# Routed experts' results: scattered to rank and token order inside the expert loop and read by plain loads, in place of rows by slot and 32 gathers

## The chip, the cores and the metric

The kernel runs on one core of a Trainium2 chip, in one launch. The metric is the device time in microseconds (us). The core's engines are TensorE (PE, matrix products), VectorE (DVE), ScalarE (ACT), GpSimd (POOL) and SyncE (SP); each works through its own instructions in order, and semaphores hold it where it needs another engine's result or a transfer. SP and ACT issue plain DMA transfers; the indirect ones (one row per index) are issued by POOL.

## The reference

Two layers run over x (2048 tokens of 256 numbers) with a second sequence of 1601 rows as context: cross attention, a mixture of experts, a second cross attention with a gate, a second mixture. The change concerns the first mixture and the start of what follows it. With `xf` the normalised rows, that mixture is

```python
def _ffn(x, w1, w2, w3):
    return jax.nn.silu(x @ w1.T) * (x @ w3.T) @ w2.T
for i in range(2):                       # two shared experts, for every token
    shared = shared + _ffn(xf, sw1[i], sw2[i], sw3[i])
logits = xf @ router_w.T + expert_bias
rw, sel = jax.lax.top_k(logits, 2)       # two of eight experts for each token
rw = jax.nn.softmax(rw)
...
out = out + cw[:, None] * _ffn(xf, e1, e2, e3)    # for each expert; cw is 0 where not chosen
out = out + shared                       # and x = x + out
```

So each token has two chosen experts, its rank 0 and its rank 1, with weights `rw`.

## The kernel before, in words

All is float32. The 2048 tokens lie in 16 tiles of 128 (`NT = 16`; token `i*128 + p` is on partition `p`), taken in 4 blocks of 4 tiles (`NB`, `BT`). `xs` holds the running x in SBUF for the whole kernel. A scheduler in the tile framework orders each engine's instructions and sets the semaphores; a tile pool with `bufs=n` rotates n buffers, and a new tile waits for the readers of the old one.

The stages around the change, with the profile's times:

- **Norm and router (180 to 228 us).** Four blocks are normalised by DVE into `h_f` (`layernorm`, line 189) and turned by PE (line 199) into `hT_f`. 32 small products give the logits (line 508). DVE finds the two best experts of each token (lines 518 and 519) and works out a slot for each pair of token and rank (`slot`, line 580). Slots are grouped by expert, each expert's group rounded up to tiles of 128: 39 tiles (`NSLOT`).
- **Scatter (228 to 315 us).** 32 indirect transfers (line 593; loop over 16 tiles `i`, then 2 ranks `k`) put rows of `h_f` into the DRAM tensor `rows_in` at their slots. It was filled with zeros before (line 412). Each scatter waits for the one before, since all write the same tensor.
- **Shared experts (190 to 374 us), beside the scatter.** `hidden(e, b)` computes for each of 4 column groups `hc` two products of 128x512 (line 614), ACT takes silu of the first (line 619), DVE multiplies by the second (line 620). `outward` multiplies by the third weight (line 629) and DVE adds to `xs` (line 632). The products of line 614 rotate through 4 banks of PSUM, two for each `hc`, so the second product of one `hc` needs DVE's line 620 of two groups earlier.
- **Routed experts (374 to 605 us).** For each of the 39 tiles of slots: load from `rows_in` (`arrive`, line 677), turn, two products with the expert's weights (`up`, line 691), turn (line 703), third product (`down`, line 711), copy out of PSUM by DVE (`rout`, line 715), store to `rows_out` by a plain transfer that ACT issues (line 716).
- **Start of the second layer (603 to 690 us).** PE projects the context (lines 219 and 232) and folds weights (lines 780 to 814). Beside that, for each block of tokens, 8 gathers (line 830, into `g`, 6 buffers) fetch the two expert rows of each token from `rows_out` by `slot`, DVE adds them to `xs` with the weights `tw` (line 835) and normalises the block into `hr` (line 189). PE turns it (line 199), ACT copies it (line 839), and PE computes the first scores against it (line 255), which ACT copies out (line 257) and DVE takes the running maximum of (`m`, line 263).

```python
for b in range(NB):                                  # lines 825 to 843, shortened
    for j in range(BT):
        i = b * BT + j
        for k in range(2):
            nc.gpsimd.indirect_dma_start(out=g, in_=rows_out, in_offset=...slot[:, k, i : i + 1]...)
            nc.vector.scalar_tensor_tensor(xs[:, i, :], g, tw[:, i, k : k + 1], xs[:, i, :], ALU.mult, ALU.add)
    h = layernorm(b * BT, BT, prew, hr[:, b * BT : (b + 1) * BT, :])
    turn_block(ps_t, h, ...)
    scores(first_em, hT, S, qs[:, :, 0:BW], BW, None, first=b * BT, end=(b + 1) * BT)
```

Of the kernel before, what the change touches and what calls it, by code (L numbers as in the profile page):

```python
# [9 lines left out]
F32 = mybir.dt.float32  # L10
# [7 lines left out]
P = 128  # L18
# [24 lines left out]
def xattn_ffn_kernel(ctx: ExitStack, tc: tile.TileContext, t: dict, out: bass.AP):  # L43
# [30 lines left out]
        return w  # L74


    rows_in = tc.dram_tile([NSLOT * P, D], F32, name="rows_in")
    rows_out = tc.dram_tile([NSLOT * P, D], F32, name="rows_out")

    rows_sub = tc.dram_tile([SC, 2 * D], F32, name="rows_sub")  # L80

# [1 line left out]
    tw = const.tile([P, NT, 2], F32, name="tw")  # L83
    slot = const.tile([P, 2, NT], U32, name="slot")
    owner = const.tile([P, NSLOT], I32, name="owner")
    zero = const.tile([P, D], F32, name="zero")
    ident = const.tile([P, P], F32, name="ident")
    ones = const.tile([P, P], F32, name="ones")

# [222 lines left out]
    with ExitStack() as ph:  # L312
# [82 lines left out]
        for b in range(NB + 1):  # L395
            new = between = None
            if b + 1 < NB:
                h = rows_before(b + 1)
            if b < NB:
                qT, past = ready.pop(b)  # L400
                e, m = em = score_tiles(pools)
                scores(em, kT, SC, qT, BW, None)
                acc = sp.tile([P, BW], F32, name="acc")

                def each(r, k0, k1, b=b, e=e, acc=acc):
                    for k in range(k0, k1):
                        if k == 1:
                            add = nc.gpsimd.tensor_tensor(acc, e[:, 0, :], e[:, 1, :], ALU.add)
                            if b == 0:
                                with tc.issue_after(add.ins):  # L410
                                    nc.gpsimd.memset(zero, 0.0)
                                nc.sync.dma_start(
                                    rows_in.rearrange("(n p) d -> p n d", p=P),
                                    zero.unsqueeze(1).to_broadcast([P, NSLOT, D]),
                                )
                        elif k:
                            nc.gpsimd.tensor_tensor(acc[:r, :], acc[:r, :], e[:r, k, :], ALU.add)

                between = shift_exp(pools, e, m, SC, BW, each)
                new = (b, e, acc, past)  # L420
            if last is None:
                project(ps_m, wv0, ctxT, 0, 3, lambda i, r, ps: copy(i, v[:r, i, :], ps))
                next(between)
                project(ps_m, wv0, ctxT, 3, 6, lambda i, r, ps: copy(i, v[:r, i, :], ps))
                next(between)
                project(ps_m, wv0, ctxT, 6, NCT, lambda i, r, ps: copy(i, v[:r, i, :], ps))
            else:
                n, e, acc, past = last
                ov = bank(ps_m)
                for k, r in enumerate(parts_of(SC)):  # L430
                    if between is not None and k in (3, 7):
                        next(between)
                    nc.tensor.matmul(ov, v[:r, k, :], e[:r, k, :], start=(k == 0), stop=(k == NCT - 1))  # L433
                oT = sp.tile([P, BW], F32, name="oT")
                nc.scalar.copy(oT, ov)
                dps = bank(ps_s)
                for j in range(BT):
                    nc.tensor.matmul(
                        dps[:, j : j + 1], acc[:, j * P : (j + 1) * P], ones[:, 0:1], start=True, stop=True
                    )  # L440
                rden = sp.tile([P, BT], F32, name="rden")
                nc.vector.reciprocal(rden, dps[:, 0:BT])
                after(n, oT, rden, past)
            if b + 1 < NB:
                ready[b + 1] = before(b + 1, h)
            last = new
# [47 lines left out]
    with ExitStack() as ph:  # L494
# [1 line left out]
        work = sbuf(ph, "f0w", 2, "right")  # L496
        acts = sbuf(ph, "f0a", 2, "right")

        h = keep.tile([P, NT, D], F32, name="h_f")
        hT = keep.tile([P, DC, S], F32, name="hT_f")  # L500
        for b in range(NB):
            hb = layernorm(b * BT, BT, work, h[:, b * BT : (b + 1) * BT, :])
            turn_block(ps_t, hb, lambda c, tp: copy(c, hT[:, c, b * BW : (b + 1) * BW], tp))

        lg_ps = bank(ps_t)[:, : NT * NE].rearrange("p (n e) -> p n e", e=NE)
# [82 lines left out]
        nc.vector.tensor_scalar(ownf, ownf, float(NE - 1), None, ALU.min)  # L588
        nc.vector.tensor_copy(owner, ownf)

        for i in range(NT):
            for k in range(2):
                nc.gpsimd.indirect_dma_start(
                    out=rows_in, out_offset=bass.IndirectOffsetOnAxis(ap=slot[:, k, i : i + 1], axis=0),
                    in_=h[:, i, :], in_offset=None, bounds_check=NSLOT * P - 1,
                )
# [73 lines left out]
    with ExitStack() as ph:  # L670
        work = sbuf(ph, "r0w", 3)
        in_tiled = rows_in.rearrange("(n p) d -> n p d", p=P)
        out_tiled = rows_out.rearrange("(n p) d -> n p d", p=P)

        def arrive(s):
            r = work.tile([P, D], F32, name="rin")
            nc.sync.dma_start(r, in_tiled[s])
            tp = bank(ps_t)
            for c in range(DC):
                nc.tensor.transpose(tp[:, c * P : (c + 1) * P], r[:, c * P : (c + 1) * P], ident)  # L680
            rT = work.tile([P, DC, P], F32, name="rT")
            nc.vector.tensor_copy(rT.rearrange("p c q -> p (c q)"), tp[:, 0:D])
            return rT

        def up(s, rT):
            e = nc.tensor.value_load(owner[0:1, s : s + 1], min_val=0, max_val=NE - 1)
            base = nc.tensor.snap(e * (DC * HID))
            ps = [bank(ps_s) for _ in range(2)]
            for w, p in zip(routed, ps):
                for c in range(DC):  # L690
                    nc.tensor.matmul(  # L691
                        p, rT[:, c, :], w[:, bass.ds(base + c * HID, HID)], start=(c == 0), stop=(c == DC - 1)
                    )
            sl = work.tile([P, HID], F32, name="rsl")
            nc.scalar.activation(sl, ps[0], AF.Silu)  # L695
            act = work.tile([P, HID], F32, name="ract")
            nc.vector.tensor_tensor(act, sl, ps[1], ALU.mult)  # L697
            return base, act

        def turn(act):  # L700
            tp = bank(ps_t)
            for hc in range(NHC):
                nc.tensor.transpose(tp[:, hc * P : (hc + 1) * P], act[:, hc * P : (hc + 1) * P], ident)  # L703
            aT = work.tile([P, NHC, P], F32, name="raT")
            nc.scalar.copy(aT.rearrange("p c q -> p (c q)"), tp)
            return aT

        def down(s, base, aT):
            y = bank(ps_m)[:, 0:D]
            for hc in range(NHC):  # L710
                nc.tensor.matmul(  # L711
                    y, aT[:, hc, :], routed[2][:, bass.ds(base + hc * D, D)], start=(hc == 0), stop=(hc == NHC - 1)
                )
            r = work.tile([P, D], F32, name="rout")
            nc.vector.tensor_copy(r, y)
            nc.scalar.dma_start(out_tiled[s], r)

        ks = l1k.tile([P, DC, SC], F32, name="ks")
        vs = l1k.tile([P, NCT, D + 1], F32, name="vs")
        kbs = l1k.tile([P, NCT], F32, name="kbs")  # L720
        rT = {s: arrive(s) for s in range(2)}
        hid, aTs = {}, {}
        for s in range(NSLOT + 2):
            if s < NSLOT:
                hid[s] = up(s, rT.pop(s))
            if 0 <= s - 1 < NSLOT:
                base, act = hid[s - 1]
                aTs[s - 1] = turn(act)
            if s + 2 < NSLOT:
                rT[s + 2] = arrive(s + 2)  # L730
            if 0 <= s - 2 < NSLOT:
                down(s - 2, hid.pop(s - 2)[0], aTs.pop(s - 2))
            if s == 4:
                ctxT = second_layer_loads()
                nc.gpsimd.memset(vs[:, :, D : D + 1], 1.0)
# [5 lines left out]
    with ExitStack() as ph:  # L741
# [9 lines left out]
        blocks = [(0, 512), (512, 512), (1024, 256), (1280, SC - 1280)]  # L751
        pre = ExitStack()
        prew = sbuf(pre, "a1l", 2)
        gath = sbuf(pre, "a1g", 6)
        fold1 = sbuf(pre, "a1f", 1)


# [65 lines left out]
        fold_weights()  # L823

        for b in range(NB):
            for j in range(BT):
                i = b * BT + j
                for k in range(2):
                    g = gath.tile([P, D], F32, name="g")
                    nc.gpsimd.indirect_dma_start(  # L830
                        out=g, out_offset=None, in_=rows_out,
                        in_offset=bass.IndirectOffsetOnAxis(ap=slot[:, k, i : i + 1], axis=0),
                        bounds_check=NSLOT * P - 1,
                    )
                    nc.vector.scalar_tensor_tensor(
                        xs[:, i, :], g, tw[:, i, k : k + 1], xs[:, i, :], ALU.mult, ALU.add
                    )
            h = layernorm(b * BT, BT, prew, hr[:, b * BT : (b + 1) * BT, :])
            turn_block(ps_t, h, lambda c, tp: nc.scalar.copy(hT[:, c, b * BW : (b + 1) * BW], tp))
# [313 lines left out]
```

## Time and profile before

| what | value |
|---|---|
| median of 9 runs (lowest to highest) | 1145.72 us (1140.7 to 1148.41) |
| the profiled execution: its time, and its span | 1146.24 us, 1144.4 us |
| mean granted TensorE clock, share of full speed | 0.967 |
| busy share of the span: PE, DVE, ACT, POOL | 93%, 47%, 29%, 27% |
| chain that ended last, by engine | PE 73%, DVE 19%, DMA 3%, ACT 2%, issue 2% |
| the 32 scatters into `rows_in`: first to last start | 228.0 to 312.5 us |
| the 32 gathers from `rows_out`: first to last start | 606.3 to 647.5 us |

The profile is of one execution, and its times run from the span's start. The execution's time is 1.84 us more than its span, and 0.5 us above the median. Views used below are the chain of waits that ended last, tables of each engine's busy time in given stretches, lists of one engine's instructions in order of time, and the waits of one tile. In a list a row has its start, its length, the engine, the line, the operation, what it writes and reads, how often it stands there, and in brackets the idle time before it with what ended it. A matmul of 128x512 in float32 stands as two records, 0.43 us apart at full clock. Ends of matmuls are modelled, so a PE that shows busy may contain a wait.

### The profile page before, as it was taken

What the parts mean: (1) busy time and instruction counts of PE and PEld (TensorE: products, weight loads), DVE (VectorE), ACT (ScalarE), POOL (GpSimd) and SP (SyncE); (2) the same over time, 40 slices, a digit from 0 to 9 for tenths busy, and PEclk for the clock granted to TensorE, in tenths of its full rate; (3) what the DMA queues carried; (4) which work ended last, traced back from release to release, by engine and by line L of the source; (5) the groups of instructions that cost most, each with busy time, mean ns of one, the idle gap of its engine ahead of it and who ended that gap; (6) DMA issues with size and microseconds to landing.
All of it is one profiled execution on the core that took longest, in us unless ns stands there. A gap on an engine that the chain in (4) does not pass through costs nothing.

```text
span 1144.4 us, 11226 instructions
## 1 busy us (share of the span) xinstructions
PE 1066.5 (93%) x3728; PEld 654.5 (57%) x3728; DVE 541.9 (47%) x1288; ACT 330.1 (29%) x542; POOL 313.2 (27%) x298
## 2 busy tenths in 40 slices
PE   6997897999999999999999999999999965999994
PEld 3653445656566566666665644465764554575773
DVE  6677889422222222222223745441415666465664
ACT  4762532210110112221123435331305500333311
POOL 1461550033300000000006506612319998100000
PEclk9998898799999999999999999999999986999997
DMA  8410006411103111111103200000013212000000
GB/s 315 136 53 1 0 1 248 193 51 47 50 28 88 58 46 47 46 46 46 46 22 88 72 1 0 19 19 37 1 42 101 65 56 83 9 10 10 1 19 19
DMA packets 38950, 63.55 MB, mean 56 GB/s; under 512 B 6189, under 2 KB 26541, under 8 KB 38894
## 3 DMA queue, kind: packets, MB, share of 16 engines
q1 hardware_dynamic: 26686, 40.02, 10.1%
q0 software_dynamic: 5632, 16.78, 4.8%
q10 hardware_dynamic: 6576, 6.03, 1.6%
q8 instruction: 31, 0.51, 0.2%
q14 instruction: 25, 0.20, 0.1%
HBM read 43.02 MB, written 19.79 MB: 55 GB/s over the span
## 4 chain that ended last, share of the span: by engine, by line
PE 73%; DVE 19%; DMA 3%; ACT 2%; issue 2%; POOL 0%; DVEq 0%; SPq 0%; POOLq 0%; ACTq 0%
PE sc L255 17%; PE sc L691 12%; PE sc L614 10%; PE mm L898 8%; PE mm L711 6%; PE mm L629 5%; DVE e L291 3%; PE mm L306 2%; PE sc L1011 2%; PE sc L860 2%; DMA g<-rows_out,slot 2%; PE tp L703 1%; DVE st L178 1%; PE mm L433 1%; DVE newton L160 1%
## 5 line engine op out<-in xcount | busy, mean ns | idle before, releaser
L691 PE MATMUL sc<-rew,rT 128*128 x312 | 140.3, 592 | 0.6 <-DMA bvs<-in_bvs_dram 0.6
L614 PE MATMUL sc<-hT_f,ew 128*128 128x512 f32 x256 | 115.8, 608 | 0.1
L306 PE MATMUL mm<-vs,e 128*128 128x257 f32 (+1 forms) x416 | 98.9, 387 | 0.0
L291 DVE TENSOR_TENSOR e<-e,tp 128x2048 f32<-128x2048 f32 (+3 forms) x48 | 86.3, 1859 | 21.0 <-PE tp L284 21.0
L691 PEld LDWEIGHTS sc<-rew,rT 128*128 128x128 f32 x312 | 59.0, 190 | 58.7 <-issue 56.8
L294 ACT ACTIVATE e<-e 128x2048 f32<-128x2048 f32 (+3 forms) x48 | 74.2, 1571 | 63.2 <-DVE e L291 62.8
L255 PE MATMUL sc<-hT,ks 128*128 128x512 f32 (+1 forms) x208 | 91.6, 597 | 0.0
L255 PE MATMUL sc<-qs,hT 128*128 128x512 f32 (+2 forms) x256 | 88.3, 501 | 2.5 <-DVE m L263 1.6
L257 ACT COPY e<-sc 128x512 f32<-128x512 f32 (+3 forms) x116 | 61.1, 536 | 101.5 <-PE sc L255 101.3
L898 PE MATMUL mm<-e,hr 128*128 128x512 f32 (+2 forms) x256 | 88.0, 499 | 0.0
L306 PEld LDWEIGHTS mm<-vs,e 128*128 128x128 f32 (+1 forms) x416 | 78.8, 194 | 13.0 <-issue 2.5
L263 DVE TENSOR_TENSOR m<-sc,m 128x512 f32<-128x512 f32 (+3 forms) x100 | 62.6, 626 | 49.6 <-ACT e L257 46.6
L697 DVE TENSOR_TENSOR ract<-rsl,sc 128x512 f32<-128x512 f32 x39 | 26.8, 687 | 120.2 <-PE sc L691 116.8
L614 PEld LDWEIGHTS sc<-hT_f,ew 128*128 128x128 f32 x256 | 49.6, 196 | 58.1 <-issue 56.7
L711 PE MATMUL mm<-rew,raT 128*128 x312 | 73.6, 379 | 0.0
L255 PEld LDWEIGHTS sc<-qs,hT 128*128 128x128 f32 x256 | 47.8, 189 | 39.1 <-issue 26.4
L898 PEld LDWEIGHTS mm<-e,hr 128*128 128x128 f32 x256 | 48.2, 190 | 35.4 <-issue 28.2
L255 PEld LDWEIGHTS sc<-hT,ks 128*128 128x128 f32 (+1 forms) x208 | 38.6, 187 | 46.9 <-issue 46.2
L255 PE MATMUL sc<-qT,kT 128*128 128x512 f32 (+1 forms) x104 | 51.4, 649 | 13.6 <-DVE m L263 13.6
L695 ACT ACTIVATE rsl<-sc 128x512 f32<-128x512 f32 x39 | 23.3, 597 | 134.3 <-PE sc L691 134.3
L796 POOL COPY wvg<-wvc 128x256 f32<-128x256 f32 x2 | 0.7, 400 | 222.7 <-PE sc L691 222.7
L711 PEld LDWEIGHTS mm<-rew,raT 128*128 128x128 f32 x312 | 56.3, 190 | 6.1
(260 smaller groups left out, 1564.0 us busy)
## 6 DMA issues: line engine op xcount, KB each, us to landing
rew<-in_ew_dram SPq DMA_DIRECT2D x24, 512.0 KB, 10.7
rows_in<-zero SPq DMA_DIRECT2D x1, 4992.0 KB, 16.2
rin<-rows_in SPq DMA_DIRECT2D x39, 128.0 KB, 2.0
rows_out<-rout ACTq DMA_DIRECT2D x39, 128.0 KB, 1.7
ew<-in_ew_dram SPq DMA_DIRECT2D x7, 512.0 KB, 8.4
ctxT<-in_ctxT_dram SPq DMA_DIRECT2D x6, 512.0 KB, 7.8
rows_sub<-sgrow SPq DMA_DIRECT2D x12, 256.0 KB, 2.0
out_dram<-xs SPq DMA_DIRECT2D x8, 256.0 KB, 2.1
```

The costliest lines, as they stand in the source:

```text
L255: nc.tensor.matmul(ps, kT[:, d, k * P : k * P + r], q[:, d, :], start=(d == 0), stop=(d == nd - 1))
L257: nc.scalar.copy(e[:r, k, :w], ps)
L263: nc.vector.tensor_tensor(m[:r, :w], ps, upto, ALU.max)
L291: nc.vector.tensor_tensor(part, part, bc[:r, :w].unsqueeze(1).to_broadcast([r, k1 - k0, w]), ALU.add)
L294: nc.scalar.activation(part, part, AF.Exp)
L306: nc.tensor.matmul(ov[:c, : D + 1], e[:r, k, j * P : j * P + c], v[:r, k, :], start=(k == 0), stop=(k == len(rows) - 1))
L614: nc.tensor.matmul(p, w[:, c, cols], hT[:, c, b * BW : (b + 1) * BW], start=(c == 0), stop=(c == DC - 1),)
L629: nc.tensor.matmul(y, act[:, hc, j * P : (j + 1) * P], a2[:, hc, :], start=(hc == 0), stop=(hc == NHC - 1))
L691: nc.tensor.matmul(p, rT[:, c, :], w[:, bass.ds(base + c * HID, HID)], start=(c == 0), stop=(c == DC - 1))
L697: nc.vector.tensor_tensor(act, sl, ps[1], ALU.mult)
L711: nc.tensor.matmul(y, aT[:, hc, :], routed[2][:, bass.ds(base + hc * D, D)], start=(hc == 0), stop=(hc == NHC - 1))
L898: nc.tensor.matmul(ov, hr[:, k, d * P : (d + 1) * P], e[:, k, :w], start=(k == 0), stop=(k == NT - 1))
```

## The change

The row of a slot now carries its destination with it. `rows_in` is one number wider (257), and so are `h_f` and `zero`. Before the scatters of rank `k`, DVE writes the integer `k*2048 + token` into the last column of `h_f`; the loop is now over `k` first, then `i`. The zero rows carry numbers from 4096 up, a dump area. When the scatters have landed, one transfer on SP reads the 4992 single numbers of that column into `goes_to`. In the expert loop POOL scatters each tile of results to `rows_out[goes_to]`, where it was stored by slot. `rows_out` is thus in order of rank and token, and each block of 512 tokens is read by two plain transfers of 512 KB on SP (`g0` and `g1`, 2 buffers each) where there were 8 gathers.

```diff
-    rows_in = tc.dram_tile([NSLOT * P, D], F32, name="rows_in")
-    rows_out = tc.dram_tile([NSLOT * P, D], F32, name="rows_out")
+    rows_in = tc.dram_tile([NSLOT * P, D + 1], F32, name="rows_in")
+    rows_out = tc.dram_tile([2 * S + P, D], F32, name="rows_out")
...
-                                    nc.gpsimd.memset(zero, 0.0)
+                                    nc.gpsimd.memset(zero[:, 0:D], 0.0)
+                                    nc.gpsimd.iota(
+                                        zero[:, D : D + 1].bitcast(I32), pattern=[[0, 1]], base=2 * S, channel_multiplier=1
+                                    )
...
-        h = keep.tile([P, NT, D], F32, name="h_f")
+        h = keep.tile([P, NT, D + 1], F32, name="h_f")
+        place_i = keep.tile([P, 2, NT], I32, name="place_i")
+        nc.gpsimd.iota(place_i, pattern=[[S, 2], [P, NT]], base=0, channel_multiplier=1)
...
-        for i in range(NT):
-            for k in range(2):
+        for k in range(2):
+            nc.vector.tensor_copy(h[:, :, D : D + 1].bitcast(I32), place_i[:, k, :].unsqueeze(2))
+            for i in range(NT):
                 nc.gpsimd.indirect_dma_start(
                     out=rows_in, out_offset=bass.IndirectOffsetOnAxis(ap=slot[:, k, i : i + 1], axis=0),
                     in_=h[:, i, :], in_offset=None, bounds_check=NSLOT * P - 1,
...
+            nc.sync.dma_start(goes_to, rows_in.rearrange("(n p) d -> p n d", p=P)[:, :, D].bitcast(U32))
...
-            nc.sync.dma_start(r, in_tiled[s])
+            nc.sync.dma_start(r, in_tiled[s][:, 0:D])
...
-            nc.scalar.dma_start(out_tiled[s], r)
+            nc.gpsimd.indirect_dma_start(
+                out=rows_out, out_offset=bass.IndirectOffsetOnAxis(ap=goes_to[:, s : s + 1], axis=0),
+                in_=r, in_offset=None, bounds_check=2 * S + P - 1,
+            )
...
-        gath = sbuf(pre, "a1g", 6)
+        gath = sbuf(pre, "a1g", 2)
+        by_token = rows_out[0 : 2 * S, :].rearrange("(k n p) d -> p k n d", k=2, p=P)
...
         for b in range(NB):
+            got = []
+            for k in range(2):
+                g = gath.tile([P, BT, D], F32, name=f"g{k}")
+                nc.sync.dma_start(g, by_token[:, k, b * BT : (b + 1) * BT, :])
+                got.append(g)
             for j in range(BT):
                 i = b * BT + j
-                for k in range(2):
-                    g = gath.tile([P, D], F32, name="g")
-                    nc.gpsimd.indirect_dma_start(
-                        out=g, out_offset=None, in_=rows_out,
-                        in_offset=bass.IndirectOffsetOnAxis(ap=slot[:, k, i : i + 1], axis=0),
-                        bounds_check=NSLOT * P - 1,
-                    )
+                for k, g in enumerate(got):
                     nc.vector.scalar_tensor_tensor(
-                        xs[:, i, :], g, tw[:, i, k : k + 1], xs[:, i, :], ALU.mult, ALU.add
+                        xs[:, i, :], g[:, j, :], tw[:, i, k : k + 1], xs[:, i, :], ALU.mult, ALU.add
                     )
```

More of the change, by code (lines that the diff above doesn't have):

```diff
@@ L85, in xattn_ffn_kernel @@
     owner = const.tile([P, NSLOT], I32, name="owner")
-    zero = const.tile([P, D], F32, name="zero")
+    goes_to = const.tile([P, NSLOT], U32, name="goes_to")
+    zero = const.tile([P, D + 1], F32, name="zero")
     ident = const.tile([P, P], F32, name="ident")
@@ L410, in each @@
                                 with tc.issue_after(add.ins):
-                                    nc.gpsimd.memset(zero, 0.0)
+                                    nc.gpsimd.memset(zero[:, 0:D], 0.0)
+                                    nc.gpsimd.iota(
+                                        zero[:, D : D + 1].bitcast(I32), pattern=[[0, 1]], base=2 * S, channel_multiplier=1
+                                    )
                                 nc.sync.dma_start(
                                     rows_in.rearrange("(n p) d -> p n d", p=P),
-                                    zero.unsqueeze(1).to_broadcast([P, NSLOT, D]),
+                                    zero.unsqueeze(1).to_broadcast([P, NSLOT, D + 1]),
                                 )
@@ L497, in xattn_ffn_kernel @@
         acts = sbuf(ph, "f0a", 2, "right")
-        h = keep.tile([P, NT, D], F32, name="h_f")
+        h = keep.tile([P, NT, D + 1], F32, name="h_f")
+        place_i = keep.tile([P, 2, NT], I32, name="place_i")
+        nc.gpsimd.iota(place_i, pattern=[[S, 2], [P, NT]], base=0, channel_multiplier=1)
         hT = keep.tile([P, DC, S], F32, name="hT_f")
         for b in range(NB):
-            hb = layernorm(b * BT, BT, work, h[:, b * BT : (b + 1) * BT, :])
+            hb = layernorm(b * BT, BT, work, h[:, b * BT : (b + 1) * BT, 0:D])
             turn_block(ps_t, hb, lambda c, tp: copy(c, hT[:, c, b * BW : (b + 1) * BW], tp))
@@ L672, in xattn_ffn_kernel @@
         in_tiled = rows_in.rearrange("(n p) d -> n p d", p=P)
-        out_tiled = rows_out.rearrange("(n p) d -> n p d", p=P)
+        with nc.allow_non_contiguous_dma(reason="one element of each row"):
+            nc.sync.dma_start(goes_to, rows_in.rearrange("(n p) d -> p n d", p=P)[:, :, D].bitcast(U32))
         def arrive(s):
             r = work.tile([P, D], F32, name="rin")
-            nc.sync.dma_start(r, in_tiled[s])
+            nc.sync.dma_start(r, in_tiled[s][:, 0:D])
             tp = bank(ps_t)
```

## The prediction

> **What bounds the kernel.** I read the page's busy times and the chain of waits first, then the tables of stretches for the stages that the diff touches, then the lists of each engine there.
>
> ```profile
> PE 1066.5 (93%) x3728; PEld 654.5 (57%) x3728; DVE 541.9 (47%) x1288; ACT 330.1 (29%) x542; POOL 313.2 (27%) x298
> ...
> PE 73%; DVE 19%; DMA 3%; ACT 2%; issue 2%; POOL 0%; DVEq 0%; SPq 0%; POOLq 0%; ACTq 0%
> ```
>
> PE is busy 93% of the span, and the diff leaves its work as it is: it takes away transfers. So the question is where PE stands still for those. The chain gives DMA 3%, which looks like the gathers; stretches of the stage with the gathers tell what that is worth (columns: length, then busy time and count of PE, weight loads, DVE, ACT, POOL; granted clock, DMA share, GB/s):
>
> ```profile
> core 0: us, PE busy (x) PEld busy (x) DVE busy (x) ACT busy (x) POOL busy (x), PEclk, DMA share, GB/s
> 604.00:612.00 8.00, 8.00 (x20) 3.46 (x19) 1.60 (x4) 3.04 (x5) 4.49 (x5) 1.00 0.22 67
> 612.00:622.00 10.00, 10.00 (x31) 4.96 (x30) 5.03 (x15) 4.31 (x8) 7.74 (x8) 1.00 0.36 105
> ...
> 652.00:662.00 10.00, 8.11 (x25) 3.80 (x24) 8.54 (x31) 3.16 (x7) 0.00 (x0) 1.00 0.00 0
> ```
>
> PE works through the gathers without a gap until the last stretch. Who held it there, by the list of its waits between 605 and 665 and the lists of PE and DVE:
>
> ```profile
> PE sc L255 <- DVE m L263: 1.6, 1, 1.6
> PE sc L255 <- ACT hT L839: 0.6, 2, 0.3
> ```
> ```profile
> 654.62 1.98 PE L255 MATMUL sc<-qs,hT 128*128 128x512 f32 x4 [0.29 <-ACT hT L839]
> 658.21 1.98 PE L255 MATMUL sc<-qs,hT 128*128 128x512 f32 x4 [1.60 <-DVE m L263]
> ```
> ```profile
> 656.17 1.38 DVE L189 TENSOR_SCALAR hr<-xs,mv,rstd 128x256 f32<-128x256 f32 x4
> 657.47 0.68 DVE L263 TENSOR_TENSOR m<-sc,e 128x512 f32<-128x512 f32 x1
> ```
>
> The gathers pace DVE (its line 835 waits for them 24 times, 22.6 us together), DVE ends its last normalisation at 657.5, and only then comes the maximum (line 263) that frees a bank for PE. PE, not the gathers, sets the rest of the stage. In the order of instructions of the changed kernel, PE's sequence here is the same.
>
> **Term A, the read-back: -1.9.** PE's two matmuls from 654.62 take four records of 0.43, so they end at 656.34; the next starts at 658.21. 1.87 is what the gathers cost. New dates: the last three scatters of results follow one another as the old ones do (a new start each 2.68). `rout` of the last three tiles is ready at 599.66 and the two that follow; starts at 599.70, 602.38, 605.06, landing by 607.7. Eight loads of 512 KB follow on SP. The zero fill moves 4992 KB in 16.2, 315 GB/s, so 1.4 to 1.7 a load, behind a landing time of 1.7 (a 128 KB store): block 0's pair is there by 611 to 612, and the others stay ahead of DVE. DVE's work from 604 to 657.5 sums to 31.5, so it is done at 643 to 645, 12 before PE needs it. It pays from the first microsecond and ends at 1.87: PE is full before, and the two stalls of 0.29 on ACT stay.
>
> **Term B, the first copy into `h_f`: +0.2, and scatters later.** The nearest row is DVE's copy of 128x32 at line 580, 0.17; I take 0.2. It stands behind the normalisations, in a stretch where DVE is the limit:
>
> ```profile
> 180.00:200.00 20.00, 15.20 (x64) 9.49 (x63) 19.73 (x115) 5.78 (x12) 1.40 (x10) 0.83 0.89 349
> ```
>
> There the order also moves one matmul of line 614 ahead of the logits (line 508). PE loses nothing by that, but the logits, and with them slots and scatters, come 0.86 later, less some idle time that it fills: I take 0.8. The first scatter starts at 228.8 instead of 228.0.
>
> **Term C, the second copy: +2.1.** The copy for `k=1` overwrites what the 16 scatters of `k=0` read, so DVE waits for their landing. In DVE's new order it stands after the eighth line 632 of the shared experts (which ends at 264.6), and queued behind it are line 620 for `hc=0` of the next group and all after it. Line 620 frees a bank that PE needs two groups on. The lists of POOL, DVE and ACT:
>
> ```profile
> 268.64 0.97 POOL L593 DMA_INDIRECT rows_in<-h_f,slot  x1 [1.70 <-DMA rows_in<-h_f,slot]
> 271.31 0.97 POOL L593 DMA_INDIRECT rows_in<-h_f,slot  x1 [1.70 <-DMA rows_in<-h_f,slot]
> ```
> ```profile
> 264.19 0.42 DVE L632 TENSOR_TENSOR xs<-xs,mm 128x256 f32<-128x256 f32 x1 [1.30 <-PE mm L629]
> 268.06 0.69 DVE L620 TENSOR_TENSOR act<-sl,sc 128x512 f32<-128x512 f32 x1 [3.45 <-PE sc L614]
> ```
> ```profile
> 272.77 0.60 ACT L619 ACTIVATE sl<-sc 128x512 f32<-128x512 f32 x1 [2.84 <-PE sc L614]
> ```
>
> The row at 271.31 is the 17th scatter, released by the landing of the 16th, which is what the copy now waits for. So the copy starts at 271.31 + 0.8 + 16d, where d is what a row of 1028 bytes adds to a scatter's 2.71 over one of 1024. Copy 0.2, line 620 0.65: the bank is free at 272.96 + 16d. PE needs it when the first product of `hc=2` is done; silu of that starts at 272.77, as soon as it is, so 272.73. Stall: 0.2 + 16d. The trace has no write that isn't aligned to 1024, so d has bounds only. Below: 0, or a little less by chance, for 4 bytes in 1024. Above: the data movement of a scatter doubled. The queue's packets fill 13.1% of 16 engines over the 90 us with the 32 scatters, 0.37 each, so d is at most 0.37 and the stall at most 6.1. I take 0.12, nearer to the row of the same scatter than to its double: 0.2 + 1.9 = 2.1.
>
> [...]
>
> **At nothing, with their cover.** The zero fill of 257 columns (46 to 62; SP's next transfer is at 181). Loads of `rin` (median 2.0), issued two tiles of 5.82 ahead. 39 scatters on POOL in place of 39 stores on ACT: 2.68 each within 5.82 a tile, `rout` has three buffers, and PE runs through this loop without a gap. `goes_to`, 4992 single numbers, waits on SP for the last scatter (about 320). By rows: above, 4992 elements at the rate at which the load of `bvT`, 256 single elements, exceeds a plain store of 128 KB (3.1 against 1.7; 16 a DMA engine, so 0.09 each) are 312 a DMA engine, 28 us, done near 348. Behind it on SP are loads of the first routed weights, due from 360.5 on. Over 45 us would delay these and PE behind them. The scatters end some 5 later than before, near 320; `rin` is first loaded at 367.8.
>
> **The sum.** 0.2 + 2.1 - 1.9 = +0.4. The profiled execution took 1146.24 (span 1144.4), so 1146.6; it is 0.5 above the median, against which the forecast is **1146.1**.
>
> **What else moves: the clock.** The delayed logits are small products, and around them the clock is granted at half:
>
> ```profile
> 208.00:212.00 4.00, 4.00 (x21) 4.00 (x20) 0.00 (x0) 0.00 (x0) 0.00 (x0) 0.50 1.03 411
> ...
> 219.00:222.00 3.00, 3.00 (x11) 1.54 (x10) 2.22 (x11) 1.43 (x2) 0.00 (x0) 0.97 0.00 0
> ```
>
> By narrower stretches the half clock lasts from 205.5 to 219.2, 13.7 us. Moving its edges costs half of the move. A quarter of the stretch, 3.4, is worth 1.7 either way, and I carry that as noise. [...]
>
> **Rivals.**
>
> *Neither sign shows (0.42):* the forecast: the gain of A and the wait of C cancel within noise; d between 0.02 and 0.24. Its own range is 1144.2 to 1148.0.
>
> *Faster (0.20).* The scatters aren't later than before and d is near 0, so the copy is through by 271.5, line 620 before 272.73, and C is 0: 0.2 - 1.9 = -1.7. With a half-clock stretch shorter by 3.4, another -1.7: 1142.3. For it: the landing of a scatter (2.4) is mostly fixed time, 0.37 being data. Against: the moved matmul eats the slack of 0.5 alone.
>
> *Slower (0.38).* The wait of DVE at the second copy takes the place of the gathers' wait: from d above 0.24 the whole is over 0.2% slower. At 0.37 C is 6.1 and the sum 0.2 + 6.1 - 1.9 = +4.4: 1150.1; with a longer half-clock stretch 1151.8. [...] Against: so small a share of a scatter's time is data.
>
> *The read-back late, or `goes_to` over 45 us* (within the 0.38): DVE's chain would have to begin after 623 instead of 611, each microsecond beyond costing one. *That the gathers were hidden anyway* is most of the forecast: 22.6 us of DVE's waits are worth 1.9.
>
> The range is 1142.3 to 1151.8, both rivals' ends. One execution of this kernel can't be told from another within 0.2%, 2.3 us: faster by more than that 0.20, within 0.42, slower 0.38.
>
> **What would show it.** In the profile after: scatters in `rows_in` start 2.71 + d apart; DVE stands idle from about 265 to the 16th landing, with PE idle before the second product of `hc=2` at 272.7; no wait of PE on line 263 near 656; loads of `g0`, `g1` land from 611 on; `goes_to` lands before 360. Wrong would be: PE waiting for `rin` or routed weights after 360, PE waiting for block 0's `hr` before 645, or a period of scatters over 3.1.

## The result, and the profile after

The changed kernel takes 1154.13 us (median of 10 runs, 1151.54 to 1157.33) against 1145.31 for the kernel before (31 runs): a ratio of 1.008, 95% interval 1.0067 to 1.0093. It is slower by 0.8%. The forecast was 1146.1, with a range of 1142.3 to 1151.8, and had called no change that can be seen the likeliest. The profiled execution took 1152.37, its span 1150.6. Its lines have other numbers; those of the kernel before stand in brackets: scores 257 (255), maximum 265 (263), the new copies 599, scatters 601 (593), products of the shared experts 622 (614), the product on DVE 628 (620), 640 (632).

First the list of PE's waits, between 185 and 380 us and then between 605 and 665:

```profile
PE sc L622 <- DVE act L628: 5.4, 1, 5.4
PE tp L201 <- DVE h_f L191: 4.6, 1, 4.6
```
```profile
PE mm L805 <- ACT vT L796: 0.5, 1, 0.5
PE mm L827 <- ACT eT L796: 0.3, 1, 0.3
PE sc L257 <- ACT hT L851: 0.3, 1, 0.3
```

The wait on the maximum, 1.6 before, is gone (the wait of 4.6 on line 191 stood there before with 4.7). In its place PE waits 5.4 on line 628 of the shared experts. The lists of POOL, DVE and PE there show the chain that was forecast:

```profile
271.28 0.97 POOL L601 DMA_INDIRECT rows_in<-h_f,slot  x1 [2.09 <-DMA rows_in<-h_f,slot]
274.75 0.97 POOL L601 DMA_INDIRECT rows_in<-h_f,slot  x1 [2.50 <-DVE h_f L599]
```
```profile
274.11 0.18 DVE L599 COPY h_f<-place_i 128x16 int32<-128x16 int32 x1 [12.69 <-DMA rows_in<-h_f,slot]
274.21 1.28 DVE L628 TENSOR_TENSOR act<-sl,sc 128x512 f32<-128x512 f32 x2
```
```profile
274.96 8.26 PE L622 MATMUL sc<-hT_f,ew 128*128 128x512 f32 x12 [5.42 <-DVE act L628]
```

DVE stands 12.69 us ahead of the copy, until the 16th scatter (row 271.28) has landed. Two of line 628, which had been queued behind the copy, then go through in one piece, and PE resumes at 274.96. The clock did something that nobody had priced. Stretches around it (PE busy, PEld, DVE, ACT, POOL, granted clock, DMA share, GB/s):

```profile
268.00:274.00 6.00, 1.54 (x4) 0.38 (x2) 0.00 (x0) 0.00 (x0) 1.94 (x2) 0.99 0.12 44
274.00:281.00 7.00, 6.04 (x8) 2.62 (x9) 2.08 (x4) 0.60 (x1) 2.15 (x3) 0.52 0.11 38
281.00:290.00 9.00, 9.00 (x39) 6.98 (x38) 1.95 (x4) 0.60 (x1) 3.27 (x4) 1.00 0.13 46
```

By narrower stretches the half clock lasts from 273.9 to 280.7, 6.8 us. It begins while PE still stands, so PE works 5.7 us at half clock (274.96 to 280.7) and loses 2.9 of them. By this profile the second copy costs 5.4 + 2.9 = 8.3.

The other dates, by differences between the two profiles: from the last copy of `rout` to line 898 (910 now) 86.5 us before, 84.9 after; the expert loop, first to last product, 220.0 in both; from the start to its first product 376.4 and 381.7. That last difference, 5.3, is less than 8.3 since the half-clock stretch at the router is 6.8 here where it was 13.7, which is worth 3.4 the other way. These sum to +5.3 - 1.6 of the 6.2 between the spans. The rest, about 2.4, lies between line 910 and the end, whose code the change leaves as it is. In the sixteen profiles of this case that last part takes 451.8 to 457.4 us, with 36.5 to 46.2 us at half clock in it, so differences of some us between single profiles say nothing on the change.

### The profile page after: what moved, and what is told of

It reads as the page before. It is cut to its first block, busy times and chain, and to the rows that moved or that the text cites. A ratio compares the mean times of both kernels' runs of the same rounds, so it can differ in the third digit from the quotient of the medians.

```text
span 1150.6 us, 11190 instructions
## 1 busy us (share of the span) xinstructions
PE 1066.5 (93%) x3728; PEld 653.4 (57%) x3728; DVE 541.9 (47%) x1290; ACT 329.7 (29%) x542; POOL 320.0 (28%) x307
## 4 chain that ended last, share of the span: by engine, by line
PE 71%; DVE 16%; issue 7%; ACT 2%; DMA 1%; POOL 1%; DVEq 0%; POOLq 0%; SPq 0%; ACTq 0%
PE sc L257 18%; PE sc L700 12%; PE mm L910 7%; PE mm L720 6%; PE sc L622 5%; PE mm L637 4%; DVE e L293 3%; PE mm L308 2%; PE sc L1023 2%; PE sc L872 2%; PE sc L221 2%; PE tp L712 1%; PE mm L438 1%; DVE newton L162 1%; POOL rows_in L601 1%
## 5 line engine op out<-in xcount | busy, mean ns | idle before, releaser
L725 POOL DMA_INDIRECT rows_out<-rout,goes_to x39 | 38.0, 973 | 196.1 <-DVE rout L724 190.5
L308 PEld LDWEIGHTS mm<-vs,e 128*128 128x128 f32 (+1 forms) x416 | 78.9, 195 | 13.1 <-issue 2.5
L257 PEld LDWEIGHTS sc<-hT,ks 128*128 128x128 f32 (+1 forms) x208 | 38.6, 187 | 46.9 <-issue 46.2
L601 POOL DMA_INDIRECT rows_in<-h_f,slot x32 | 31.4, 981 | 106.2 <-DMA rows_in<-h_f,slot 60.5
## 6 DMA issues: line engine op xcount, KB each, us to landing
rew<-in_ew_dram SPq DMA_DIRECT2D x24, 512.0 KB, 10.2
rows_in<-zero SPq DMA_DIRECT2D x1, 5011.5 KB, 21.6
```

The lines of the kernel that those rows point to most:

```text
L257: nc.tensor.matmul(ps, kT[:, d, k * P : k * P + r], q[:, d, :], start=(d == 0), stop=(d == nd - 1))
L308: nc.tensor.matmul(ov[:c, : D + 1], e[:r, k, j * P : j * P + c], v[:r, k, :], start=(k == 0), stop=(k == len(rows) - 1))
L601: nc.gpsimd.indirect_dma_start(out=rows_in, out_offset=bass.IndirectOffsetOnAxis(ap=slot[:, k, i : i + 1], axis=0), in_=h[:, i, :], in_off ...
```

## Experiments

The kernels ran in four groups, each on a chip of its own together with the kernel before. On the first two chips that one took 1145.7 and 1145.1 us, on the last two 1160.6 and 1160.8; a ratio is always to the kernel before on the same chip.

**The second copy on POOL.**

```diff
-            nc.vector.tensor_copy(h[:, :, D : D + 1].bitcast(I32), place_i[:, k, :].unsqueeze(2))
+            (nc.gpsimd if k else nc.vector).tensor_copy(h[:, :, D : D + 1].bitcast(I32), place_i[:, k, :].unsqueeze(2))
```

> The changed kernel with one difference: the second copy into h_f (rank 1) runs on POOL, in its queue between the 16th and 17th scatter, so DVE waits for nothing there. Theory A (DVE's wait at that copy holds the bank, and the standstill of 5.4 us then costs a stretch of half clock): the scatters still start 3.0 us apart, but PE has no wait on line 628 and no half clock between 273 and 281; 5.4 + 3.4 = 8.8 us less than the changed kernel, 1143.5 to 1146 us, level with the kernel before. Theory B (the loss lies in the expert loop, in 39 scatters of results, or in the wider rows themselves): 1152 us or more. Theory C (only the standstill counts, the half clock would come anyway): 1148 to 1149.

Measured: 1146.65 us, ratio 0.9997 (0.9981 to 1.0013). PE has no wait between 200 and 340, and the same two stretches are full:

```profile
268.00:274.00 6.00, 6.00 (x17) 2.84 (x16) 0.99 (x2) 1.19 (x2) 1.78 (x3) 1.00 0.13 47
274.00:281.00 7.00, 7.00 (x33) 5.94 (x32) 2.07 (x5) 0.00 (x0) 2.92 (x3) 1.00 0.11 38
```

The scatters themselves are as slow as in the changed kernel (3.08 for the first 16). So the loss, the half clock too, hangs on DVE's wait, to within the interval of 0.16% (1.8 us) either way. The 39 scatters in the expert loop cost nothing there: the loop takes 220.0 us in all sixteen profiles, with scatters or with stores. The strided load and the wider rows cost nothing that shows. The median is 0.65 above theory A's range, with single runs from 1140.8 to 1147.9.

**The scatter side alone.**

```diff
-            nc.gpsimd.indirect_dma_start(out=rows_out, out_offset=...goes_to[:, s : s + 1]..., in_=r, ...)
+            nc.scalar.dma_start(out_tiled[s], r)
...
-                nc.sync.dma_start(g, by_token[:, k, b * BT : (b + 1) * BT, :])
+                    nc.gpsimd.indirect_dma_start(out=g, in_=rows_out, in_offset=...slot[:, k, i : i + 1]...)
```

> The scatter side of the change alone: wide rows, rank order and both copies on DVE stay, goes_to is loaded, but the results are stored by slot by ACT and read back by the 32 gathers as before. Theory A: PE's standstill of 5.4 and the half clock behind it are there as in the changed kernel, and the wait of 1.6 to 1.9 on line 265 near 656 is back: 1.9 us slower than the changed kernel, 1155 to 1157 us. Theory B (scatters of results cost something in the expert loop): faster than the changed kernel, under 1153. If the read-back was worth more than 1.9, over 1158.

Measured: 1152.9 us (6 runs), ratio 1.0068 (1.0051 to 1.0084). In the profile both waits are there, though not of the size that theory A has: 6.5 on line 628 and 1.3 on line 265, with 6.8 us of half clock at the first. The median misses: it is 1.2 below the changed kernel where 1.9 above was expected, and so just in theory B's range. What theory B would need, a longer expert loop with scatters, isn't there (220.0 us in both). The profiled execution, of 1155.8, lies in theory A's range. A gain of under 2 us can't be read from these medians.

**Rows of 272 numbers, and of 264.** Both widen `rows_in`, `h_f` and `zero`, so that each scatter writes the wider row whole, and leave the rest, the wait of DVE included.

```diff
-    rows_in = tc.dram_tile([NSLOT * P, D + 1], F32, name="rows_in")
+    rows_in = tc.dram_tile([NSLOT * P, 272], F32, name="rows_in")
```

> The changed kernel with rows of 272 numbers (1088 bytes, a multiple of 64) in rows_in, h_f and zero instead of 257 (1028 bytes); everything else as in the changed kernel, DVE's wait at the second copy too. Theory A1 (rows that begin at odd addresses land later): the scatters start 2.70 to 2.75 us apart again, the 16th lands some 4.5 us earlier against PE, PE waits under 1 us on line 628, no half clock behind it: 1143.5 to 1146.5. Theory A2 (any row longer than 1024 bytes lands later): the period stays at 3.0 or grows, 1153 or more. Theory A3 (64 bytes is not enough, only 256 or 512 would do): period 2.9 to 3.0, 1152 or more.

> The changed kernel with rows of 264 numbers (1056 bytes, a multiple of 32 but not of 64). Theory A1 with a step at 64 bytes: period of the first 16 scatters 2.9 to 3.0 as with 1028 bytes, PE waits some 5 us on line 628. With a step at 32 bytes or less: 2.70 to 2.75 and under 1 us. Theory A2: 3.0.

Measured with 272: 1142.91 us, 0.6 below the expected range, ratio 0.9989 (0.9976 to 1.0002); period of the first 16 scatters (from one start to the next) 2.73 instead of 3.04. With 264: 1144.73 in one run, period 2.73. PE's waits, first with 272 and then with 264:

```profile
PE sc L622 <- DVE act L628: 0.5, 1, 0.5
```
```profile
PE sc L622 <- DVE act L628: 0.6, 1, 0.6
```

More bytes per row, and the landing is early again, so the amount of data isn't it. Rows of 1056 bytes, a multiple of 32 and not of 64, are enough for the 2.73. Most rows of 1028 bytes neither begin nor end on multiples of 32 in DRAM; which of the two counts isn't shown, since rows that begin 1056 bytes apart with only 1028 of them written weren't run. What became longer shows in the issues and shares of DMA, first of the kernel before (225 to 315 us), then of the changed one (222 to 322):

```profile
q0 software_dynamic: 1536, 4.20, 13.1%
...
rows_in<-h_f,slot POOLq DMA_INDIRECT x32, 2.4
```
```profile
q0 software_dynamic: 1536, 4.21, 11.9%
...
rows_in<-h_f,slot POOLq DMA_INDIRECT x32, 2.7
```

13.1% of 90 us and 11.9% of 100 us, over 32 scatters, are 0.37 us each in both. In these scatters the engines move rows of 1028 bytes as fast as those of 1024; the time from issue to landing grows, from 2.4 to 2.7 in the median. The zero fill grew too: 16.2 us in rows of 1024 bytes, 20.4 to 21.6 in rows of 1028, 17.2 in rows of 1088. But there it is the engines' own time: between 44 and 70 us the fill's queue has 58.6% of the 16 engines before and 76.9% after, 15.2 and 20.0 us.

**Which side.** `h_f` padded to 264 in SBUF, `rows_in` and the length of what is written left at 257.

```diff
-        h = keep.tile([P, NT, D + 1], F32, name="h_f")
+        h = keep.tile([P, NT, 264], F32, name="h_f")
...
-                    in_=h[:, i, :], in_offset=None, bounds_check=NSLOT * P - 1,
+                    in_=h[:, i, 0 : D + 1], in_offset=None, bounds_check=NSLOT * P - 1,
```

> The changed kernel with h_f padded to 264 numbers in SBUF, while each scatter still moves 257 numbers into rows_in of 257: the rows begin at multiples of 32 bytes on the reading side only. If the writing side makes the landing later: period 2.95 to 3.1 and PE waits 5 to 6.5 us on line 628. If the reading side does: 2.70 to 2.75 and under 1 us.

Measured: period 3.14, PE's wait 6.9, 1155.56 us in one run. Rows that begin at multiples of 32 bytes on the reading side alone didn't help; it took the writing side, in DRAM, for the period of 2.73.

**More scatters ahead of the copy.** With rows of 264, a repeat of the first scatter (the same rows once more) before the second copy, once or twice:

```diff
+            for _ in range(1 if k else 0): nc.gpsimd.indirect_dma_start(out=rows_in, out_offset=...slot[:, 0, 0:1]..., in_=h[:, 0, :], ...)
             nc.vector.tensor_copy(h[:, :, D : D + 1].bitcast(I32), place_i[:, k, :].unsqueeze(2))
```

> Rows of 264 numbers (period 2.73, wait 0.6 in the run before) and one scatter more ahead of the second copy: the 16 scatters of rank 0 are followed by a repeat of the first one, so DVE waits for 17 landings. Theory A (stall = landing of the last one + 0.85 - PE's need): PE's wait on line 628 is 0.6 + 2.7 = 3.3 us. Theory B (the standstill had another cause than the number of landings that DVE waits for): 0.6 as before. Clock: if 3.3 us of standstill are enough for a stretch of half clock, one begins between 272 and 280; theory A holds either way.

> As the run with one scatter more, but two: DVE waits for 18 landings. Theory A: 0.6 + 5.4 = 6.0 us on line 628, and a half clock of 6.8 us behind it, as with the 5.4 us of the changed kernel. Theory B: 0.6 and none.

Measured: waits of 0.3 and 3.2, at 1140.79 and 1148.36 us. Both expectations missed by 3, and the list of DVE (here with two more) says why: the scheduler put the copy behind one line 628 more.

```profile
264.15 0.69 DVE L628 TENSOR_TENSOR act<-sl,sc 128x512 f32<-128x512 f32 x1 [3.45 <-PE sc L622]
274.63 0.18 DVE L599 COPY h_f<-place_i 128x16 int32<-128x16 int32 x1 [9.79 <-DMA rows_in<-h_f,slot]
```

What is now held up is the line 628 of the next column group, whose bank PE needs 3.43 us later (two products of 1.716). 0.6 + 2.7 - 3.4 is about 0, and 0.6 + 5.4 - 3.4 = 2.6; the period was 2.77 in these runs instead of 2.73, which over 16 scatters adds 0.7 to each: 0.6 and 3.3 against the measured 0.3 and 3.2. So the formula fits to 0.3 once the copy's place and the period are read from these runs; that is a fit after the fact, not a forecast that came true. A dose of the clock came with it, in the run with two more:

```profile
276.00:280.00 4.00, 4.00 (x9) 2.36 (x8) 0.71 (x2) 0.12 (x1) 1.27 (x2) 0.57 0.20 72
```

With the standstill of 3.2 us came 3.4 us at half clock, all of them after it (1.7 lost). With those of 5.4 to 6.9 came 6.8, which begin 1.1 to 2.3 us before PE resumes, so 2.2 to 2.9 are lost. With those of 0.3 to 0.6 came none. In all five profiles with a half clock at this wait, it begins 4.3 to 4.8 us after PE stopped.

**Both remedies at once.** Rows of 264, both copies on POOL.

```diff
-    rows_in = tc.dram_tile([NSLOT * P, D + 1], F32, name="rows_in")
+    rows_in = tc.dram_tile([NSLOT * P, 264], F32, name="rows_in")
...
-            nc.vector.tensor_copy(h[:, :, D : D + 1].bitcast(I32), place_i[:, k, :].unsqueeze(2))
+            nc.gpsimd.tensor_copy(h[:, :, D : D + 1].bitcast(I32), place_i[:, k, :].unsqueeze(2))
```

> Both remedies at once: rows of 264 numbers, and both copies into h_f on POOL, so that neither stands in DVE's stretch before 200 nor makes DVE wait. Theory A: what is left of the change is the read-back without the gathers, 1.7 us less than the kernel before (from the last copy of rout to line 910: 84.9 us against 86.6): 1143.5 to 1144.5, a ratio near 0.9985. Rival (the read-back gives nothing that lasts to the end): a ratio of 1.000. Slower than 1.001 would speak against both.

Measured: 1144.92 us, ratio 0.9995 (0.9984 to 1.0006). No standstill is left, the stage of the read-back lasts 84.9, and yet the time is level with the kernel before; the interval holds both 0.9985 and 1.000.

**Plain loads against gathers, nothing else different.** To get at the read-back, the kernel with both remedies and its twin with stores by slot and 32 gathers (the edit of the scatter side alone, on rows of 264) ran on one chip, with the unchanged kernel before as a third.

> What the read-back alone is worth where nothing else stands still: rows of 264 numbers and both copies on POOL, but results stored by slot and the 32 gathers kept. Theory A: the stage from the last copy of rout to the first product of line 911 lasts 86.6 us as before, against 84.9 with plain loads, and the kernel takes 1.7 us more than the one with plain loads of the same call: level with the kernel before, ratio 1.000. Rival (the gain of 1.7 is taken back later, by the clock of the second layer): the same time as with plain loads although the stage differs.

> The kernel with both remedies once more, on the chip of the run with gathers: theory A has it 1.7 us under that one and under the kernel before (0.9985); the rival has all three level. Its profile gives a second set of the half-clock stretches after 900 us, which differ from run to run.

> The kernel before, unchanged, for a second profile of it: the stage with the gathers lasts 86.6 us again if that is fixed; the length of the half-clock stretch at the router's products (13.7 us in the first profile) and those after 900 us differ if they are a matter of phase.

Measured: 1161.79 with gathers, ratio 1.0012 (0.9989 to 1.0034); 1144.47 with loads, ratio 0.9856 (0.9826 to 0.9885); 1161.69 in one run of the kernel before. None of the expectations had a difference of 17 us. The loads take what they took on the other chips; it is the two kernels with gathers that are 16 us slower here. In the kernel before the stage from `rout` to line 898 now lasts 102.4 instead of 86.5. A fourth group, on a fourth chip, looks at that.

> Rows of 264, both copies on POOL, plain loads. On a chip where ACT doesn't stand still during gathers: 1.7 us under its twin with gathers (theory A), or level with it (rival: the second layer's clock takes the gain back). On a chip where it does: some 16 us under it, with 1144 to 1146 of its own either way.

> Its twin with results stored by slot and 32 gathers. Without standstills of ACT during the gathers: level with the kernel before, 1145 to 1147. With them: 1160 or more, and the rows of ACT at line 774 show idle time of 5 to 8 us before them.

> The changed kernel once more: PE waits 5 to 7 us on line 628 and gets a stretch of half clock behind it, and the read-back has no gathers. On a chip without standstills of ACT during gathers 8 to 9 us over the kernel before, as at first; on one with them 6 to 8 us under it (16 less, less 8.8).

Measured: 1145.52 with loads, ratio 0.9877 (0.9851 to 0.9902); 1161.31 with gathers, ratio 1.0012 (0.9996 to 1.0028); 1152.86 for the changed kernel, ratio 0.9942 (0.9921 to 0.9963), with a wait of 6.0 on line 628 and its half clock. The waits of PE between 600 and 700, and rows of ACT, in the kernel with gathers:

```profile
PE sc L234 <- ACT qs L774: 8.1, 1, 8.1
PE sc L221 <- ACT qs L774: 4.8, 1, 4.8
```
```profile
626.63 0.69 ACT L774 ACTIVATE qs<-sc,fbias_c 128x512 f32<-128x512 f32 x1 [5.73 <-remote]
635.84 0.69 ACT L774 ACTIVATE qs<-sc,fbias_c 128x512 f32<-128x512 f32 x1 [8.52 <-issue]
```
```profile
622.00:632.00 10.00, 1.69 (x9) 1.34 (x7) 5.74 (x26) 0.69 (x1) 7.56 (x9) 0.64 0.32 93
632.00:642.00 10.00, 5.42 (x13) 4.32 (x14) 4.91 (x26) 2.54 (x8) 5.79 (x6) 0.50 0.25 75
```

In 622 to 642, while POOL issues gathers, ACT stands for 5.7 and 8.5 us ahead of two activations, PE with it (1.7 busy of 10), and the clock falls to half. "remote" and "issue" name no releaser that the profile knows. ACT isn't alone, and it needn't be the first: in the profile of the kernel before from the third chip PE's own waits have no releaser either, and DVE stands too.

```profile
PE sc L232 <- issue: 10.3, 2, 6.4
```
```profile
640.64 0.17 DVE L154 TENSOR_SCALAR seed<-ve 128x4 int32<-128x4 int32 x1 [5.59 <-remote]
```

The two profiles with gathers from the chips of 1145 us have no such rows. What holds these engines there is open: the gathers' packets fill the DMA engines as on the first chip (24.5% of 600 to 660 us there in a second profile of the kernel before, 24.0% in the first). That fewer gathers in flight, or gathers earlier, would avoid it wasn't tried. Nor is the chip told apart from the occasion: each chip served one group only, and the two groups with slow gathers are also the last two in time.

## Why the prediction was wrong

**The bound and the gathers: right where the kernel before takes 1145 us.** PE was the bound, the wait on line 265 is gone, and the stage is 1.6 us shorter in every profile with plain loads (84.9 against 86.5), where 1.87 was worked out. In whole kernels it couldn't be told from zero on these chips (0.9995, 0.9984 to 1.0006). Its dates slipped: the last scatter of results starts at 613.9, 8.8 later than worked out, of which 5.3 is the later loop. Most of the rest is one scatter that landed late: POOL stands 4.5 us ahead of the next. So the loads are issued from 616.4, and DVE ends at 650.4, not 645. PE had slack for that.

**The first copy and the delayed scatters: right, or too small to see.** 0.18 for 0.2. The delay of the scatters can't be told from the clock: the first one starts between 224.6 and 230.2 in the nine profiles of kernels with this copy on DVE, where the half-clock stretch at the router lasts 6.8, 10.2 or 13.7 us. In the changed kernel's profile it is 6.8 and the start 225.7, for a forecast of 228.8: the noise that was carried as 1.7 either way, an estimate, here twice that.

**The second copy: the chain of waits right in each step, the size wrong.** This is the term that failed: 2.1 was forecast, and 5.4 came, plus a half-clock term of 2.9 that the sum didn't have. The stall is 0.2 + 16d as worked out (d is what the wider row adds to a scatter's period), but d is 0.33 in that profile, and 0.37 to 0.43 in four others with rows of 1028 bytes, where 0.12 was taken and 0.37 was the upper bound. With 0.33 the formula gives 5.5 against 5.4 measured. The value was picked from the data movement of a scatter, on the ground that four bytes in 1024 can't add much to it. They don't: 0.37 stayed 0.37. What grew was the rest of the time from issue to landing (2.4 in the median before, 2.7 after), which had been taken as fixed. So the bound from doubled data movement bounded the wrong thing, and that 0.33 lies below it is luck: 0.43 was measured too. Nor does it take a boundary of 256 or 512 bytes, as theory A3 had it: rows of 1056 and 1088 bytes, of which most don't begin on one, had a period of 2.73 against 2.71 for those of 1024.

**What was left out: the clock after the stall.** The prediction moved half-clock stretches about and never asked whether its own stall would make one; it put this at nothing without a reason. The profile before had something like it: PE stands 4.7 us at line 199, from 183.6 to 188.2, and the clock is at half from 185.1 to 191.9 (0.50 granted in 186 to 189). In the changed kernel the standstill of 5.4 us costs 2.9 more. With d of 0.33 and that term the sum would have been 0.2 + 5.5 + 2.9 - 1.9 = +6.7, against +8.8 measured (7.7 to 10.7). In the three other profiles with this stall, waits of 6.0 to 6.9 and their half clock come to 8.8 to 9.2, which would make it 7.1 to 7.5. So 1 to 2 us stay open. That the 1.6 of the read-back doesn't last to the end, as the kernel with both remedies allows, would fit that; it isn't shown.

**The rivals.** The slower one, at 0.38, was the case: "the wait of DVE at the second copy takes the place of the gathers' wait", with the turning point at d of 0.24. It ended at 1151.8, below what was measured, because the clock's term was missing, and in other profiles because d went past its upper bound. `goes_to`, feared up to 28 us, landed in 5.6; the late read-back, `rin` and the routed weights cost nothing.

**"That the gathers were hidden anyway" doesn't hold everywhere.** It holds in the profile that the forecast was made from. On two other chips the same gathers go with 16 us more, and on the one of them where the changed kernel ran it is faster by 0.6%, with its stall and all.

## What to carry to other kernels

Before a wait is put into an in-order engine, look at what its queue will hold up. Here the wait in DVE's queue cost what stood behind it, from the landing of the last transfer it waited for (5.4 us of PE), and PE's standstills of 3.2 to 6.9 us there came with 3.4 to 6.8 us of half clock on top; given to POOL, which waits for that transfer anyway, it cost nothing that shows (0.9997, 0.9981 to 1.0013). Don't widen rows in DRAM by one number: at 264 instead of 257 the same scatters landed 0.3 us earlier each. And time a kernel on more than one chip, and more than once, before a gather is called hidden: the version with both remedies is level with the kernel before on one chip and 1.2 to 1.4% faster on two others.

## What the runs showed that was not expected

Scatters into rows of 1028 bytes had a period of 3.04 to 3.14 us against 2.71 to 2.78 for 1024, 1056 and 1088, with the same 0.37 us of engine time for 1024 and 1028. It took the DRAM side to mend that; with rows that begin at multiples of 32 bytes in SBUF alone it was 3.14. A load of 4992 single numbers landed in 4.5 to 6.0 us. A standstill of PE of 3.2 us came with 3.4 us of half clock, one of 5.4 to 6.9 with 6.8, which begin before PE resumes. And 32 gathers that were hidden on two chips went with standstills of ACT, DVE and PE of 5 to 9 us on two others, 16 us in all, from a cause that the profile doesn't name.
